# A four-layer graph network: graph 0's first attention row without the identity, graph 2's first layer placed earlier, and a new order of all steps

## The chip, the cores and the metric

The kernel runs on one core of a Trainium2 chip. Its engines are TensorE (PE, matrix products; weight loads are shown apart as PEld), VectorE (DVE), ScalarE (ACT), GpSimd (POOL) and SyncE (SP); the last two and ACT also start DMA transfers. Every engine takes its instructions in order, and an instruction that waits for a semaphore holds those behind it on the same engine. The metric is the time of one execution on the device, in microseconds; lower is better. The time before is the median of three runs.

## The reference

Sixteen independent graphs of 1024 nodes with 128 features pass through four layers. All four use the same 0/1 adjacency matrix of the graph, and each ends with a residual and a normalization:

```python
x = _layernorm(x + _L0_gnn_ref(x, adj, W, a))                     # one attention head, 128 wide
x = _layernorm(x + _L1_gnn_ref(x, adj, adj, W, a))                # 8 heads of 16, ELU at the end
x = _layernorm(x + _L2_gnn_ref(x, adj, rel_weights, self_w, ...)) # mean over neighbours, own norm
x = _layernorm(x + _L3_gnn_ref(x, adj, W))                        # 4 heads of 32, scores Wh.Wh
```

Layer 0 is the layer that the change touches most:

```python
H = X @ W;  s = H @ a_src;  t = H @ a_dst
e = leaky_relu(s[:, None] + t[None, :], 0.2)
attention = softmax(where(A > 0, e, -1e9));  out = relu(attention @ H)
```

The kernel writes the exponential of a leaky ReLU as a maximum of two products. With `most`, the largest t, each weight is proportional to max(R0[i], q[j]) times a factor of j alone, where R0[i] = exp(-0.8 max(s[i] + most, 0)) and q[j] = exp(0.8 (t[j] - most)). So a mask product needs a tile R0 that holds the row over i on all 128 partitions, a number q per partition, and the mask. Layer 1 does the same with eight heads.

## The kernel before, in words

The fast path is `tile_binary`; `tile_general` stands behind a branch that is taken only if the adjacency is not 0/1, and does not run here. A graph has eight masks (`m`, 128 source nodes by 1024 targets, 8-bit floats), which POOL loads and converts by DMA (L605).

`before0` loads the transposed features in two chunks (`xT`, L621), multiplies them with `w0c` (`products`, L393: W and, as extra columns, W a_src, W a_dst and -1/128), copies the result to `hd` on ACT (L629, L636), takes the largest t on DVE (L643) and over the partitions on POOL (L416), and forms `r` (L654, exponential at L660) and `q`. For graph 0 the tile R0 is made by 16 matmul records (L585) whose weights are columns of `r` and whose other operand is the identity matrix. For all other graphs the row goes through DRAM: a transpose with the identity (L498), a copy (L500), a store (L503) and a load to all partitions (L672). `layer0` then makes, for each half of the targets, eight mask products on DVE (L697, 128x512) and the sums on PE (L709), and divides, adds the residual and normalizes (`layernorm`, L438 to L486).

`before1` and `layer1` do the same for eight heads in two groups of four: 64 mask products of 128x1024 per graph (L849) and the sums (L857, four heads side by side in PE's columns). Graph 0's first four R tiles are again made by products with the identity (L585) and ACT copies (L810), the rest by DMA (L814). `last1` applies ELU, residual and norm. `layer2` sums over neighbours on PE with the mask as weights (L989) and has its own norm. `before3` prepares layer 3, and `layer3` computes scores on PE (L1139 for the missing edges, L1150), exponentials on ACT (L1221) and sums on PE (L1165; in the last graphs L1176 and L1187, with additions on DVE at L1243).

The order of the work is not that of the code. Every piece is a `step` with an engine, an estimated duration, a due time and the buffers that it reads and writes. `Plan.run` walks through time: per engine it takes, among the steps that can start within `WINDOW` of the first possible start, the one with the smallest due time, emits its instructions, and so fixes the engine's order. For PE a step of the same tiling mode as the last one (full, rows, 32 columns) counts as due `SAME` earlier. `lag` is the delay that the plan assumes until others see the result, for a DMA its landing. Pools hold a fixed number of places, and a step that needs a place waits until one is free. `plan.user("acc1", due, ...)` gives the turns on the one pair of accumulators that layers 0 and 1 share: graph 0's layer 0 (0), graph 1's (25), graph 0's layer 1 in two groups (99 and 154.5), graph 1's first group (228), graph 2's layer 0 (258), graph 1's second group (283.5), and so on, 129 apart.

The identity (`constants`, L512 to L535) is made in DRAM by three transfers that depend on each other, issued by ACT (L525): zeros, ones on the diagonal, and the load to `b_ident`. `far`, a scaled copy for layer 3, follows on DVE (L535). `weights` loads and prepares the weights.

Of the kernel before, what the change touches and what calls it, by code (L numbers as in the profile page):

```python
# [28 lines left out]
P = 128  # L29
HALF = 512  # L30
# [46 lines left out]
class Plan:  # L77
# [8 lines left out]
    SAME = 43.42  # L86
    WINDOW = {"DVE": 0.32, "ACT": 0.56, "POOL": 24.74, "SP": 1.21, "PE": 0.04}
    URGENT = 87.13
# [145 lines left out]
def tile_binary(  # L234
# [62 lines left out]
    LATER1 = 126.77  # L297
    LATER3 = -19.68
    LATERX = 258.97
# [43 lines left out]
    places("x1", 2, [P, NB, P])  # L343
    places("x2", 2, [P, NB, P])
    places("x3", 2, [P, NB, P])
# [40 lines left out]
    def products(xT, w, due, into, us, floor=0.0):  # L386
# [14 lines left out]
        step("PE", us, due - 42.13, emit, [xT, w], [out], holds=[into], floor=floor)  # L401
        return out, lambda: out.t.rearrange("p (k c) -> p k c", c=SLOT)[:, :, :cols]

    def turned(x_nat, chunk, due):

        pt, xT = Buf("wk", "pt"), Buf("xTc", "xTc")
        step(
            "PE", 0.44, due - 52.2, lambda: transposes(pt.t, [x_nat.t[:, chunk * HB + k, :] for k in range(HB)]),
            [(x_nat, chunk), xT, identity], [pt],
        )  # L410
        step("ACT", 0.47, due + 19.59, lambda: nc.scalar.copy(xT.t, pt.t[:, :HALF]), [pt], [xT])
        return xT

    def over_partitions(v, op, shape, due, op_us=None):
        got = little(f"all{shape[1]}", shape)
        step("POOL", 0.6 if op_us is None else op_us, due - 256.91, lambda: nc.gpsimd.partition_all_reduce(got.t, v.t, P, op), [v, heated], [got], lag=0.6)  # L416
        return got

    def sums(y, half, tot, due):

        ks = slice(half * HB, (half + 1) * HB)
        step(
            "DVE", 0.62, due - 13.18, lambda: nc.vector.tensor_reduce(tot.t[:, ks], y.t[:, ks, :], AX.X, ALU.add),  # L423
            [(y, half)], [(tot, half)],
        )

    def layernorm(y, tot, due, rest=None, half=None):
# [16 lines left out]
        step("DVE", 0.1, due - 236.47, minus_mean, [tot_of, rest] if rest else [tot_of], [off])  # L444
# [7 lines left out]
        for pair in pairs:  # L452
            step(
                "ACT", 1.05, due + pair - 6.55, lambda pair=pair: square(pair), [off, (y, pair // 2)], [(squared, pair), junk]
# [5 lines left out]
            "ACT", 0.17, due - 65.07,  # L460
# [4 lines left out]
            "ACT", 0.17, due - 217.77,  # L465
# [3 lines left out]
            "DVE", 0.1, due - 138.7,  # L469
# [12 lines left out]
        step("DVE", 0.35, due - 474.69, newton, [about, var, off], [rstd, shift])  # L482
# [7 lines left out]
        for pair in pairs:  # L490
            step("ACT", 0.77, due + pair - 6.15, lambda pair=pair: apply(pair), [shift, rstd], [(y, pair // 2)])

    def rows_everywhere(r, flat, count, due):
# [4 lines left out]
            "PE", 0.2, due + 269.89, lambda: nc.tensor.transpose(pt.t[: count * NB, :P], flat(r.t), ident), [r, rT, identity], [pt]  # L498
        )
        step("ACT", 0.2, due - 282.01, lambda: nc.scalar.copy(rT.t[: count * NB, :], pt.t[: count * NB, :P]), [pt], [rT])  # L500
        step(
            "SP", 0.5, due - 721.27,
# [7 lines left out]
    def load(due, into, out, in_, part=None):  # L510
        step("SP", 0.45, due - 48.89, lambda: nc.sync.dma_start(out=out(), in_=in_), [], [(into, part)], lag=3.0)

    def constants(due):
        none = Buf("z", "none")
        step("DVE", 0.2, due - 932.32, lambda: nc.vector.memset(none.t[:, :P], 0.0), [], [none])
        for n, (out_, in_) in enumerate(
# [7 lines left out]
                "ACT", 0.1, due - 1208.47,  # L524
                lambda out_=out_, in_=in_: nc.scalar.dma_start(out=out_(), in_=in_()),  # L525
                [none] if n == 0 else [square_of] if n == 2 else [], [square_of] if n < 2 else [identity], lag=2.5,
            )
            if n == 0:

                def table():  # L530
                    nc.scalar.preload_act_table_set("natural_log_exp_and_others")
                    nc.scalar.activation(warm, warm, AF.Exp)

                step("ACT", 1.5, due - 840, table, [], [heated])
        step("DVE", 0.2, due - 74.81, lambda: nc.vector.tensor_scalar(far, ident, -FAR, None, ALU.mult), [identity], [farther])  # L535
        step(
            "POOL", 0.5, due - 989.31, lambda: nc.gpsimd.partition_all_reduce(warm, warm, P, bass_isa.ReduceOp.add),
# [3 lines left out]
    def weights(due):  # L541
        t = Buf("z", "prep")
        load(due - 1904.86, w0c, lambda: w0c.t[:, :P], w0, 0)
        load(due - 1680.94, t, lambda: t.t[:, : 2 * P], a0.rearrange("k o -> (k o)").partition_broadcast(P), 0)
# [8 lines left out]
        step("DVE", 0.9, due - 280.19, joined0, [(t, 0)], [w0c, (t, 1)])  # L553
        due += 90
        u = Buf("z", "prep")
        load(due - 65.18, w1c, lambda: w1c.t[:, :P].rearrange("p (h o) -> p h o", h=H1), w1.rearrange("h f o -> f h o"), 0)
        load(due + 386.63, u, lambda: u.t[:, : 2 * P], a1.rearrange("h k o -> (h k o)").partition_broadcast(P), 0)
# [10 lines left out]
        step("DVE", 1.1, due - 112.88, joined1, [(u, 0)], [w1c, (u, 1)])  # L568
        due += 60
        load(due - 435.76, w2c, lambda: w2c.t[:, P:], w2[1], 0)  # L570
        load(due - 69.23, u, lambda: u.t[:, 4 * P : 5 * P], self_w, 2)
        load(due - 442.33, rows["self_b"], lambda: rows["self_b"].t, self_b.partition_broadcast(P))
        pt = Buf("wk", "pt")
        step("PE", 0.2, due + 255.16, lambda: transposes(pt.t, [u.t[:, 4 * P : 5 * P]]), [(u, 2), identity], [pt])
# [1374 lines left out]
```

## Time and profile before

| what | value |
|---|---|
| median of 3 runs | 2183.86 us (2183.72 to 2184.57) |
| the profiled execution, own time | 2186.08 us |
| its span in the profile | 2184.2 us |
| PE busy, DVE busy, ACT busy | 2046.5, 1945.6, 1761.7 us |
| mean granted PE clock | 0.978 |
| first mask product of layer 0 | 24.67 us after the span's start |
| first mask product of layer 1 | 67.75 us |
| layer 1's mask products (L849), 1024 of them | 1248.2 us of DVE, 1278 ns each as recorded |

A line of a timeline gives start, duration, engine, source line, operation, output and inputs with their shapes, how many instructions are merged, and in brackets how long the engine was idle before and what ended that idle time. A line by stretch gives the length, busy time and number of instructions for PE, PEld, DVE, ACT and POOL, then the granted PE clock as a share, the DMA engines' busy share and GB/s. A line of the list of waits gives who waited for whom, with the sum in us, how often, and the longest. Records of PE overlap, since matmuls are pipelined, so the start of the next group tells more than a group's duration.

### The profile page before, as it was taken

How to read it: one execution, taken by the hardware profiler on the slowest of the kernel's cores; microseconds unless marked ns; L12 is line 12 of the kernel's file. 1: busy time of each engine (PE TensorE's matmuls, PEld its weight loads, DVE VectorE, ACT ScalarE, POOL GpSimd, SP SyncE). 2: the span in 40 equal slices, each digit the busy share in tenths (PEclk: the TensorE clock that was granted, in tenths of full speed). 3: DMA queues.
4: the chain of work that ended last, by engine and by line, in shares of the span. 5: the costliest groups of instructions: out<-in, count | busy, mean ns of one | idle time of the engine just before them, and what ended most of it. 6: DMA issues, size and time to landing. Idle time of an engine off the chain costs nothing.

```text
span 2184.2 us, 55248 instructions
## 1 busy us (share of the span) xinstructions
PE 2046.5 (94%) x23344; PEld 982.0 (45%) x23344; DVE 1945.6 (89%) x2883; ACT 1761.7 (81%) x4360; POOL 109.8 (5%) x185
## 2 busy tenths in 40 slices
PE   6757999999999999999999999999999999999877
PEld 5414445453544545354454435345443635442422
DVE  5799999999999999999999999999999999999444
ACT  3414769889797979979797997979799797979987
POOL 1000000000000000000000000000000000000000
PEclk9888999999999999999999999999999999999989
DMA  7140220412323041232204122220413222020000
GB/s 114 49 98 20 65 60 15 101 38 86 43 79 57 18 100 34 86 43 93 44 18 101 33 91 38 93 43 18 101 33 91 38 91 38 2 78 11 11 2 22
DMA packets 81282, 119.97 MB, mean 55 GB/s; under 512 B 7560, under 2 KB 59136, under 8 KB 81024
## 3 DMA queue, kind: packets, MB, share of 16 engines
q1 hardware_dynamic: 62160, 99.43, 13.7%
q0 software_dynamic: 18432, 16.79, 9.5%
q8 instruction: 184, 3.01, 0.6%
q14 instruction: 74, 0.61, 0.1%
q10 hardware_dynamic: 432, 0.13, 0.0%
HBM read 157.61 MB, written 9.04 MB: 76 GB/s over the span
## 4 chain that ended last, share of the span: by engine, by line
PE 47%; DVE 29%; issue 15%; ACT 5%; DMA 2%; POOL 1%; POOLq 0%; SPq 0%; DVEq 0%; ACTq 0%
DVE z L849 18%; PE acc L709 10%; PE acc L1165 10%; PE acc L857 9%; PE wk L1150 6%; PE wk L384 3%; PE wk L393 3%; PE wk L1139 2%; POOL all L416 1%; PE wk L1062 1%; DMA R<-rows 1%; DVE tot L423 1%; PE acc L1176 1%; DVE rest L957 1%; DVE x L964 1%
## 5 line engine op out<-in xcount | busy, mean ns | idle before, releaser
L849 DVE SCALAR_TENSOR_TENSOR z<-R,q,m 128x1024 f32<-128x1024 f32 x1024 | 1248.2, 1278 | 23.0 <-PE acc L857 20.7
L857 PE MATMUL acc<-z,hh 128*32 128x512 f32 x4096 | 516.7, 613 | 59.4 <-DVE z L849 57.0
L1221 ACT ACTIVATE z<-wk,low 128x1024 f32<-128x1024 f32 x448 | 477.8, 1108 | 29.8 <-PE wk L1150 27.5
L1165 PE MATMUL acc<-z,hh 128*32 128x512 f32 x1792 | 454.3, 598 | 1.7 <-ACT z L1221 1.7
L1165 PE MATMUL acc<-z,ones 128*32 128x512 f32 x1792 | 454.3, 598 | 0.0
L448 ACT ACTIVATE junk<-x,off 128x128 f32<-128x128 f32 x640 | 257.1, 402 | 42.8 <-DVE off L442 26.7
L1150 PE MATMUL wk<-whT,turn 32*64 32x512 f32 x3952 | 287.0, 615 | 0.0
L857 PEld LDWEIGHTS acc<-z,hh 128*32 128x32 f32 x4096 | 117.5, 111 | 367.0 <-issue 226.8
L486 ACT ACTIVATE x<-x,shift,rstd 128x128 f32<-128x128 f32 x640 | 264.6, 487 | 6.8 <-DVE shift L480 6.6
L709 PE MATMUL acc<-hd,z 128*128 128x129 f32 x2048 | 252.3, 279 | 8.2 <-DVE z L697 4.3
L709 PEld LDWEIGHTS acc<-hd,z 128*128 128x128 f32 x2048 | 240.7, 194 | 38.4 <-DVE z L697 16.7
L1165 PEld LDWEIGHTS acc<-z,hh 128*32 128x32 f32 x1792 | 89.6, 109 | 213.2 <-issue 181.7
L697 DVE SCALAR_TENSOR_TENSOR z<-R,q,m 128x512 f32<-128x512 f32 x240 | 165.9, 744 | 22.0 <-DMA R<-rows 22.0
L989 PEld LDWEIGHTS <-m 128*128 128x128 fp8e5 x3072 | 178.4, 98 | 14.4 <-issue 14.4
L989 PE MATMUL wk<-y,m 128*128 128x128 bf16 (+1 forms) x2976 | 175.7, 220 | 0.9 <-DVE y L975 0.9
L1129 ACT ACTIVATE gap<-m,neg_one 128x512 bf16<-128x512 fp8e5 x240 | 171.4, 716 | 0.0
L1139 PEld LDWEIGHTS <-far 32*32 32x32 bf16 x4096 | 37.1, 87 | 217.0 <-issue 214.3
L448 ACT ACTIVATION_READ_ACCUMULATOR junk<-x,off 128x1 f32 x640 | 120.8, 189 | 0.0
L1165 PEld LDWEIGHTS acc<-z,ones 128*32 128x32 f32 x1792 | 89.5, 109 | 53.1 <-issue 53.1
L1139 PE MATMUL wk<-gap,far 32*32 32x512 bf16 x3784 | 106.7, 386 | 5.7 <-ACT R L1221 5.4
L605 POOL DMA_DIRECT2D m<-in_adj_dram x128 | 68.4, 539 | 723.6 <-ACT gap L1129 698.3
L660 ACT ACTIVATE r<-r 128x8 f32<-128x8 f32 x16 | 3.3, 208 | 119.7 <-DVE r L654 119.7
(158 smaller groups left out, 2120.7 us busy)
## 6 DMA issues: line engine op xcount, KB each, us to landing
R<-rows SPq DMA_DIRECT2D x139, 512.0 KB
m<-in_adj_dram POOLq DMA_DIRECT2D x128, 128.0 KB, 5.3
xT<-in_xT_dram SPq DMA_DIRECT2D x32, 256.0 KB
x<-in_x_dram SPq DMA_DIRECT2D x16, 512.0 KB
out_dram<-x SPq DMA_DIRECT2D x15, 512.0 KB
rows<-rT SPq DMA_DIRECT2D x16, 32.0 KB
out_dram<-x SPq DMA_DIRECT2D x2, 256.0 KB
z<-in_L_gnn_a_dram SPq DMA_DIRECT2D x2, 128.0 KB
```

The source lines that it names most:

```text
L448: nc.scalar.activation(junk.t, y.t[:, k, :], AF.Square, bias=off.t[:, k : k + 1], accum_out=squared.t[:, k : k + 1])
L486: nc.scalar.activation(y.t[:, k, :], y.t[:, k, :], AF.Identity, bias=shift.t[:, k : k + 1], scale=rstd.t[:, k : k + 1])
L697: nc.vector.scalar_tensor_tensor(z.t[:, (j % 2) * HALF : (j % 2 + 1) * HALF], in0=R0.t[:, cols], scalar=q.t[:, j : j + 1], in1=m[j].t[:, c ...
L709: nc.tensor.matmul(av[k // 2].t.rearrange("p (k c) -> p k c", k=2)[:, k % 2, : P + 1], lhsT=z.t[:, at : at + P], rhs=hd.t[:, j, : P + 1], ...
L849: nc.vector.scalar_tensor_tensor(z.t, in0=G["R"][h].t, scalar=q.t[:, j, h : h + 1], in1=m[j].t, op0=ALU.max, op1=ALU.mult)
L857: nc.tensor.matmul(av[half].t[32 * c : 32 * c + 32, :], lhsT=hh.t[:, j, at : at + 32], rhs=zs[c].t[:, half * HALF : (half + 1) * HALF], st ...
L989: nc.tensor.matmul(ps.t[:, k * SLOT : k * SLOT + part.stop - part.start], lhsT=m[j].t[:, rows_i], rhs=y2.t[:, j, part], start=j == 0 and n ...
L1129: nc.scalar.activation(gap.t, m[j].t if b == B - 1 else m[j].t[:, cols], AF.Square, bias=neg_one, accum_out=squares[:, at : at + 1], satur ...
L1139: nc.tensor.matmul(sc[h // 2].t[c * 32 : (c + 1) * 32, (h % 2) * HALF : (h % 2 + 1) * HALF], lhsT=far[rows_r, rows_r], rhs=gap.t[rows_r, c ...
L1150: nc.tensor.matmul(sc[h // 2].t[r * 64 : (r + 1) * 64, (h % 2) * HALF : (h % 2 + 1) * HALF], lhsT=turns[j // HB].t[rows_h, j % HB * P + r ...
L1165: nc.tensor.matmul(av[g].t[at : at + 32, :], lhsT=lhsT, rhs=z.t[:, h, :], start=j == 0, stop=j == NB - 1,)
L1221: lambda g=g, sc=sc, zs=zs: nc.scalar.activation(zs[g].t.rearrange("p h n -> p (h n)"), sc[g].t, AF.Exp, bias=low.t, scale=S3),
```

## The change

It does five things.

- Graph 0's R0 is computed straight from the features: a matmul whose weights are the column W a_src, repeated 128 times, against the transposed features gives s on all partitions in PSUM (`straight`); DVE adds the maximum, ACT takes the exponential. The tile lies in the pool `R`, no longer in PSUM, and the identity is not used for it.
- The identity's three transfers are issued by SP, behind the loads of the features, and the lags that the plan assumes for them are longer.
- Graph 2's layer 0 gets the turn after graph 1's on the accumulators (due 50), ahead of graph 0's layer 1. Its masks are loaded after the maximum of graph 1.
- The pools `x1`, `x2` and `x3` of two places each become one pool `x` of five.
- Graph 0's layer 1 starts a group of four heads only when all four R tiles of the group are written, and the R tiles of its second group are loaded in the order that a tile of the first group allows. Nearly every due time, `SAME`, `WINDOW`, `URGENT`, the `LATER` constants and the period of the due times change too.

```diff
-    SAME = 43.42
-    WINDOW = {"DVE": 0.32, "ACT": 0.56, "POOL": 24.74, "SP": 1.21, "PE": 0.04}
-    URGENT = 87.13
+    SAME = 95.7
+    WINDOW = {"DVE": 0.33, "SP": 0.35, "ACT": 0.47, "POOL": 29.09, "PE": 0.02}
+    URGENT = 85.48
...
-    LATER1 = 126.77
-    LATER3 = -19.68
-    LATERX = 258.97
+    LATER1 = -3.66
+    LATER3 = 290.53
+    LATERX = 593.46
...
-    places("x1", 2, [P, NB, P])
-    places("x2", 2, [P, NB, P])
-    places("x3", 2, [P, NB, P])
+    places("x", 5, [P, NB, P])
...
             step(
-                "ACT", 0.1, due - 1208.47,
-                lambda out_=out_, in_=in_: nc.scalar.dma_start(out=out_(), in_=in_()),
-                [none] if n == 0 else [square_of] if n == 2 else [], [square_of] if n < 2 else [identity], lag=2.5,
+                "SP", 0.4, -900 + 4 * n + 36.19,
+                lambda out_=out_, in_=in_: nc.sync.dma_start(out=out_(), in_=in_()),
+                [none] if n == 0 else [square_of] if n == 2 else [], [square_of] if n < 2 else [identity], lag=(3.0, 4.0, 4.0)[n],
             )
...
-                    after, [m], lag=(5.0 + j if j < 4 else 1.6 + 1.05 * j) if b == 0 else 8.0 + 1.05 * j if b == 1 else 5.6,
-                    floor=0.0 if b < 2 else 124 * b - 110 + 5 * j,
+                    after, [m], lag=(4.5 + 1.2 * j if j < 4 else 1.0 + 1.05 * j) if b == 0 else 8.7 + 1.05 * j if b < 3 else 5.6,
+                    floor=0.0 if b < 3 else 124 * b - 110 + 5 * j,
                 )
-        if b == 1:
-            masks(range(NB), due + 40, [G["after"]])
+        if b in (1, 2):
+            masks(range(NB), due + 40, [graphs[b - 1]["most"]])
...
+            if b == 0:
+                step(
+                    "PE", 0.9, -700 + chunk - 130.27,
+                    lambda xT=xT, chunk=chunk: nc.tensor.matmul(
+                        straight.t[:, chunk * HALF : (chunk + 1) * HALF],
+                        lhsT=w0c.t[:, P : P + 1].to_broadcast([P, P]),
+                        rhs=xT.t,
+                        start=True,
+                        stop=True,
+                    ),
+                    [xT, w0c], [(straight, chunk)],
+                )
...
-            R0 = G["R0"] = Buf("wk", "R0_0")
+            R0 = G["R0"] = Buf("R", "R0_0")
             for half in range(2):
+                cols = slice(half * HALF, (half + 1) * HALF)
                 step(
-                    "PE", 1.0, due - 320.62 + half - 13.03, row_by_products(lambda: r.t, R0, range(half * HB, half * HB + HB)), [r, identity], [(R0, half)]
+                    "DVE", 0.7, -900 + half - 574.39,
+                    lambda cols=cols: nc.vector.tensor_scalar(
+                        R0.t[:, cols], straight.t[:, cols], most.t, 0.0, ALU.add, ALU.max
+                    ),
+                    [(straight, half), most], [(R0, half)],
+                )
+                step(
+                    "ACT", 0.6, -900 + half + 2.31,
+                    lambda cols=cols: nc.scalar.activation(R0.t[:, cols], R0.t[:, cols], AF.Exp, scale=-(1.0 - SLOPE)),
+                    [], [(R0, half)],
                 )
...
-            plan.user("acc1", (25 if b == 1 else 129 * b) + half * 10, av, made)
+            plan.user("acc1", (25 if b == 1 else 50 if b == 2 else 129 * b) + half * 10, av, made)
...
-                [kept], [R], lag=2.0, floor=75.0 if b == 0 else 0.0,
+                [kept, *G["R"][h - G1 : h - G1 + 1]] if b == 0 else [kept], [R], lag=2.0,
...
-                            lambda j=j, c=c, z=z, f=weights: f(j, c, z), [G["R"][g * G1 + c], q, m[j]], [z],
+                            lambda j=j, c=c, z=z, f=weights: f(j, c, z), (G["R"][g * G1 : g * G1 + G1] if b == 0 else [G["R"][g * G1 + c]]) + [q, m[j]], [z],
...
-    PERIOD = 131.1
+    PERIOD = 136.19
...
-        at0 = 25 if b == 1 else at
+        at0 = 25 if b == 1 else 50 if b == 2 else at
```

## The prediction

> **What bounds the kernel now.** First the page: the busy sums, and the span in 40 slices of 54.6 us.
>
> ```profile
> PE 2046.5 (94%) x23344; PEld 982.0 (45%) x23344; DVE 1945.6 (89%) x2883; ACT 1761.7 (81%) x4360; POOL 109.8 (5%) x185
> ...
> PE   6757999999999999999999999999999999999877
> ...
> DVE  5799999999999999999999999999999999999444
> ...
> PEclk9888999999999999999999999999999999999989
> ```
>
> TensorE (PE) works 2046.5 of 2184.2 us. Its 137.7 us of idleness lie in the first four slices and the last three; the first stretch also has a lower granted clock. Next, busy time by stretch (columns: length, then busy us of PE, PEld, DVE, ACT, POOL, then PEclk, DMA share, GB/s). I cut at the first mask product of layer 0 (24.67), the end of graph 1's layer 0 (64.8), the end of graph 0's layer 1 (157), and graph 0's first scores of layer 3 (about 240).
>
> ```profile
> 0.00:24.67 24.67, 9.73 (x49) 8.84 (x49) 3.39 (x19) 6.62 (x23) 8.33 (x24) 0.86 0.86 142
> 24.67:64.80 40.13, 34.68 (x283) 33.70 (x284) 26.80 (x52) 18.54 (x72) 1.84 (x4) 0.96 0.44 68
> 64.80:157.00 92.20, 57.94 (x386) 21.72 (x388) 86.90 (x88) 24.03 (x70) 6.70 (x10) 0.83 0.36 86
> 157.00:240.00 83.00, 61.04 (x517) 40.20 (x513) 78.12 (x122) 47.38 (x149) 0.90 (x1) 0.86 0.06 18
> 240.00:1985.00 1745.00, 1721.26 (x20183) 822.69 (x20175) 1642.96 (x2432) 1495.09 (x3703) 88.76 (x144) 1.00 0.25 59
> 1985.00:2184.20 199.20, 161.89 (x1940) 54.89 (x1936) 107.45 (x174) 170.10 (x347) 3.24 (x3) 0.93 0.03 10
> ```
>
> PE idles 14.9, 5.5, 34.3 and 22.0 us in the first four (76.7 together), 23.7 in the long middle, 37.3 in the tail. From 64.8 to 240 VectorE (DVE) is the bound (165.0 of 175.2 us); in the middle PE is (98.6%). So a microsecond is won by giving PE work before 240, by closing the middle's small gaps, or in the tail.
>
> Third, the timeline of the front, DVE then ACT, and who waits in the first 25 us:
>
> ```profile
> 17.10 0.23 DVE L535 TENSOR_SCALAR far<-b_ident 128x128 bf16<-128x128 f32 x1 [9.93 <-DMA b_ident<-square]
> 18.10 0.15 DVE L643 TENSOR_REDUCE top<-hd 128x1 f32<-128x8 f32 x1
> 24.67 6.68 DVE L697 SCALAR_TENSOR_TENSOR z<-wk,q,m 128x512 f32<-128x512 f32 x10 [1.20 <-PE wk L585]
> 38.17 4.73 DVE L697 SCALAR_TENSOR_TENSOR z<-R,q,m 128x512 f32<-128x512 f32 x7 [0.47 <-DMA R<-rows]
> 12.95 0.33 ACTq L525 DMA_DIRECT2D b_ident<-square  x1
> 13.38 0.60 ACT L629 COPY hd<-wk 128x520 f32<-128x520 f32 x1
> 22.30 0.22 ACT L660 ACTIVATE r<-r 128x8 f32<-128x8 f32 x1
> ```
>
> ACT's copies stand behind its identity transfer, which waits for the one before; the maximum stands behind `far`, which waits for the identity; r's exponential stands behind graph 1's copies. Graph 1's own row arrives only at 38.17.
>
> **The change, part by part.** Durations are of this execution: span 2184.2, own time 2186.08, 2.2 above the median of 2183.86. I sum against 2186.08 and take 2.2 off at the end.
>
> *Front of graph 0.* Removed from the path: the identity, r's exponential, 16 products L585 (2.05 us), three DMA issues on ACT (0.33 to 0.35 each). Added: two matmuls of 512 columns (0.63 each by L1062) beside the copies, two DVE steps of 0.69 (L964, also from PSUM), two exponentials of 0.59 (L411's size). New path: products end 12.11 (8.71 + 3.40), last copies 0.8, so 13.0; maximum and all-reduce 0.63 (18.10 to 18.73), so 13.6; one DVE step and one exponential 1.3, some 0.4 of handover: first z at 15.3, not 24.67, that is 9.4 earlier. But masks 4 to 7 still wait for the maximum. Their four issues now took 3.9 to 8.2 us to land; issued 13.5 to 15.2, the last is there by 23.4, where z j=7 wants it at 15.3 + 7 x 0.68 = 20.1. That returns 3.3: I take 6 us (ends 0 and 9.4).
>
> *The identity behind it on SP.* SP issues it after four loads (2.6). The three transfers took 5.08, 6.42 and 4.43; with issues it lands near 18.9, not 17.1. SP waits between them, and graph 1's feature loads (13.33 now) stand behind: about +1 (0 to +3). The first users, graph 1's row transpose (24.77) and `far` (first scores, 240), cover it. If `far` or the weight preparation still stands before R0's steps on DVE, the 6 us are gone.
>
> Here a rule speaks against the change: the Trainium skill's "DMA: Bandwidth & Descriptors", Issuing engines are not separate DMA queues, says that a DMA started from another engine uses the same 16 engines, so only issue time is saved. By the rule, this edit is worth ACT's three issues, 1 us, and the sum below would be 5 us poorer at the first z. The rows show the larger price: ACT's first copy is at 13.32, right behind the issue that waited.
>
> *Graph 2's masks.* Eight issues move on POOL from 124.39 (4.25 us) to behind graph 1's (to 29.2). The all-reduce at 61.84 is the next that matters, so POOL covers them. The POOL-issued DMA takes 9.5% of 2184 us for 128 masks, 1.6 us each: 13 us more in a DMA system that is busy until about 41 us. Masks are then in by about 54, just before they are used; R0 of graph 1 competes with them and lands at 34 to 41 (38.17 now). So graph 1's layer 0 starts at 38 as now, and the 6 us are given back there.
>
> *Graph 2's layer 0.* It leaves 212 to 234 and comes before layer 1 of graph 0. A layer 0 takes about 18.5 us of wall (25.47 to 43.9), 16 x 0.68 + 1.9 = 12.8 us of DVE and 16.5 of PE. What covers it: now nothing of layer 1 can start until 67.75, because graph 0's chain (residual, norm, products, rows) takes 24 us from the end of its layer 0 at 43.9. With graph 1 at 38 to 56 and graph 2 at 56 to 74, DVE is done with graph 2's z by about 72, so layer 1 starts 4.5 us later (ends 0 and +9). The new rule that graph 0's layer 1 wants all four R rows costs up to 73.07 - 67.75 = 5.3 us, but those rows are then ready before 72; layer 2's products and others are not touched. Behind it, 157 to 240 loses 12.8 us of DVE in a stretch where DVE is 94% busy, but also PE's filler. If DVE sets the chain from layer 1's end to the first scores, the stretch shrinks by 12.8; if latency sets it, DVE makes ten more z of layer 1, whose PE work of 5 us is then done early. I take 8.5, between the two. Front in all: +4.5 - 8.5 = -4 (ends: +9 - 5 = +4; 0 - 13 = -13).
>
> *The new order in the middle.* Every due time, `SAME` and the windows differ. One period:
>
> ```profile
> 614.44:741.12 126.68, 125.07 (x1470) 60.40 (x1466) 118.86 (x177) 109.80 (x274) 6.66 (x11) 1.00 0.25 60
> 741.12:867.32 126.20, 124.81 (x1470) 60.38 (x1466) 119.13 (x177) 109.65 (x274) 6.66 (x11) 1.00 0.27 60
> 867.32:994.49 127.17, 125.07 (x1470) 60.40 (x1466) 118.85 (x177) 109.78 (x274) 6.66 (x11) 1.00 0.26 60
> ```
>
> PE idles 1.4 to 2.1 us per period. A group of L857 of 8 starts its successor after 0.97 us (629.76 to 630.73), one of 16 after 1.85 (636.75 to 638.60), so a separate run costs 0.09; there are 24 such runs between the 16 score runs. `SAME` at 95.7 for 43.42 favours merging; I take three or four merged runs, 0.3, and 0.1 of idleness: -0.4 us x 13.8 periods (1745 / 126.5) = -5.5. Ends: all idleness and eight merges, -2.1 x 13.8 = -29; and every period as the worst shown, 127.17 - 126.45, +0.7 x 13.8 = +10.
>
> *Tail and pool.* The order of the last 199 us changes too; no row says which way: 0, ends -10 and +10 (PE waits of 3 to 4 us, three of them, either way). Five shared residual tiles for six: a graph's three live about 170, 110 and 226 us of a 126.5 us period, 4.0 at a time on average: 0 (up to +4 if the fifth is late).
>
> Sum: 2186.08 - 4 - 5.5 = 2176.6; less 2.2, 2174.4. I say 2174.5.
>
> **Rivals.** *Front and middle both pay in full:* the 157 to 240 stretch shrinks by all 12.8 and the period by 0.8: -13 - 11 = -24, about 2160. For it: DVE's 94% there. Against: layer 3's preparation is a chain of small steps.
>
> *The front is given back, the order is neutral:* graph 1's row keeps the start at 38.17, the +4.5 cancels the stretch behind. About 2184. For it: that wait's releaser is a DMA. Against: 34.3 us of PE idleness that earlier work can use.
>
> *Slower:* the period grows, because in the new order layer 0's R row comes late in every period. Thirteen such waits of DVE sum to 21.5 us in the middle (`DVE z L697 <- DMA R<-rows: 21.5, 13, 2.4`), and in the periods where PE has no backlog it follows. At +0.3 a period the front's 4 us are eaten; at +0.7, with the front's bad end (+4), it is 2184 + 10 + 4 = 2198. Against it: DVE has 7.6 us of slack per period.
>
> **How the numbers follow.** A measurement of this kernel tells about 0.2% (4.4 us) from no change: faster is under 2179.5, slower over 2188.2. Forecast 0.42, its own range 2163 to 2182 (0.04 of it within 0.2%); both in full 0.18; given back 0.10; slower 0.30. So faster 0.38 + 0.18 = 0.56, same 0.14, slower 0.30. The range leaves out a third of the full case, below 2154, and a third of the slower case, above 2198.
>
> **What would show it.** Right: L697 first at 15 to 19; graph 1's at 36 to 40; six layer-0 halves before the first L849, which starts at 70 to 74; first scores by 240; PE idle before 240 at 70 to 74 us; period 126.1. Wrong: `far` or a mask before L697 with a DMA as releaser past 20; first scores after 248; a period off by over 0.5 us either way, which by 13.8 outweighs all of the front; or a tail other than 199 us by over 10.

## The result and the profile after

The changed kernel took 2195.64 us (median of 6 runs, 2193.01 to 2198.83), the kernel before 2183.76 us beside it on the same chip (6 runs). The ratio is 1.0059, with an interval of 1.0046 to 1.0071: 0.6% slower, where 0.4% faster was forecast. The profiled execution took 2194.87 us, its span is 2193.1 us. The medians differ by 11.9 us and the two profiled spans by 8.9, since the profiled execution of the kernel before was 2.3 us above its median and that of the changed one 0.8 below. Lines have moved: L697 is now L718, L709 L730, L849 L870, L857 L878, L393 L391, L535 L532, L525 L523, L672 L693.

Busy sums and slices of 54.8 us, from the page of the changed kernel:

```profile
PE 2049.4 (93%) x23332; PEld 982.7 (45%) x23332; DVE 1942.4 (89%) x2884; ACT 1749.1 (80%) x4361; POOL 117.6 (5%) x185
...
PE   4856799999999999999999999999999999999887
...
DVE  2799998999999999999999999999989999999544
...
PEclk7978899999999999999999999999999999999999
```

TensorE (PE) idles 143.7 us, 6.0 more than before, and is busy 2.9 us longer. In the first slice PE's digit fell from 6 to 4, that of VectorE (DVE) from 5 to 2 and the granted clock's from 9 to 7. By stretch, cut at the first mask product of layer 0, the first of layer 1, the end of graph 0's layer 1, the first scores, and ahead of the last 199.2 us:

```profile
0.00:20.66 20.66, 6.82 (x20) 4.67 (x20) 3.90 (x15) 4.29 (x11) 8.34 (x23) 0.89 0.88 124
20.66:98.47 77.81, 57.93 (x453) 56.45 (x454) 40.84 (x87) 40.08 (x148) 6.77 (x14) 0.83 0.52 102
98.47:190.00 91.53, 57.38 (x378) 21.72 (x377) 86.63 (x87) 20.70 (x64) 1.33 (x1) 0.81 0.13 47
190.00:270.50 80.50, 55.85 (x467) 27.32 (x467) 75.01 (x106) 41.02 (x119) 1.25 (x1) 0.81 0.12 40
270.50:1993.90 1723.40, 1706.50 (x20074) 816.81 (x20078) 1626.72 (x2414) 1471.69 (x3667) 97.93 (x144) 1.00 0.25 58
1993.90:2193.10 199.20, 164.93 (x1968) 55.77 (x1952) 109.28 (x178) 171.32 (x355) 1.98 (x3) 0.94 0.03 10
```

Layer 0 starts 4 us earlier than before (20.66 for 24.67), layer 1 starts 30.7 us later (98.47 for 67.75), the first scores come 29.7 us later (270.5 for 240.8). The stretch between the end of graph 0's layer 1 and the scores is 80.5 us long for 83.8: 3.3 shorter, not 8.5.

For a ledger of the whole I cut at the issue of graph 0's and graph 11's output, which both kernels have. First the kernel before, then the changed one:

```profile
0.00:401.30 401.30, 321.21 (x3060) 175.36 (x3064) 348.37 (x493) 225.51 (x621) 26.64 (x50) 0.92 0.30 66
401.30:1792.80 1391.50, 1374.69 (x16086) 664.33 (x16082) 1307.97 (x1948) 1206.94 (x3004) 73.23 (x121) 1.00 0.26 60
1792.80:2184.20 391.40, 350.63 (x4206) 142.34 (x4198) 289.29 (x444) 329.30 (x737) 9.89 (x14) 0.96 0.11 26
```

```profile
0.00:429.70 429.70, 331.14 (x3131) 177.11 (x3131) 353.83 (x499) 231.71 (x633) 26.97 (x51) 0.88 0.28 63
429.70:1810.90 1381.20, 1372.28 (x16098) 664.55 (x16095) 1304.73 (x1948) 1195.76 (x3004) 82.10 (x121) 1.00 0.26 60
1810.90:2193.10 382.20, 345.99 (x4126) 141.07 (x4126) 283.83 (x439) 321.63 (x726) 8.53 (x13) 0.97 0.10 25
```

Front +28.4, middle -10.3, tail -9.2: together +8.9, the whole difference of the spans. The counts say more. Ahead of graph 0's output the new order does 5.5 us more of DVE's work and 71 more PE instructions; the tail has 5.5 us and 80 fewer. So I read some 5 to 6 us of the front's loss and of the tail's gain as one piece of work counted on the other side. PE's idleness went from 80.1 to 98.6 us in the front, from 16.8 to 8.9 in the middle and from 40.8 to 36.2 in the tail. The rest of the front's loss, 9.9 us, is PE busy for longer: it has the 71 instructions more, and its granted clock there is 0.88 for 0.92.

Where the front goes wrong, in the timeline of the changed kernel:

```profile
10.90 0.17 DVE L654 TENSOR_REDUCE top<-hd 128x1 f32<-128x8 f32 x1 [4.64 <-ACT hd L640]
...
11.38 4.25 POOL L602 DMA_DIRECT2D m<-in_adj_dram  x8
...
11.26 2.82 SPq L706 DMA_DIRECT2D x<-in_x_dram  x1
14.18 1.73 SPq L620 DMA_DIRECT2D xT<-in_xT_dram  x1
16.00 0.51 SPq L523 DMA_DIRECT2D b_ident<-square  x1
...
17.50 0.49 DVE L560 TENSOR_TENSOR z<-z,w1c 128x128 f32<-128x128 f32 x2 [6.44 <-DMA w1c<-in_L_gnn_W_dram]
...
20.66 0.75 DVE L718 SCALAR_TENSOR_TENSOR z<-R,q,m 128x512 f32<-128x512 f32 x1 [0.76 <-ACT q L696]
34.31 0.23 DVE L532 TENSOR_SCALAR far<-b_ident 128x128 bf16<-128x128 f32 x1 [12.90 <-DMA b_ident<-square]
...
32.87 2.09 PE L391 MATMUL wk<-w0c,xT 128*128 128x131 f32 x8 [19.75 <-DMA xT<-in_xT_dram]
36.37 2.08 PE L391 MATMUL wk<-w0c,xT 128*128 128x131 f32 x8 [1.41 <-DMA xT<-in_xT_dram]
38.25 5.40 PE L730 MATMUL acc<-hd,z 128*128 128x129 f32 x40
...
55.11 4.07 DVE L718 SCALAR_TENSOR_TENSOR z<-R,q,m 128x512 f32<-128x512 f32 x6 [3.84 <-DMA R<-rows]
```

The maximum is 7.2 us earlier (10.90 for 18.10). It releases not only graph 0's masks 4 to 7 but, behind them on POOL, graph 1's eight, all at 11.4 to 23.3 us. In that time SP's queue holds graph 0's rows of x (512 KB, issued at 11.26), the first half of graph 1's features (256 KB, 14.18) and the identity (64 KB, 16.00). Before, the features were issued at 13.33 and the rows behind them, at 14.38; the new order has the rows in front. The features are in use 18.7 us after their issue (they took 4.4 before), the identity 18.3 (at most 4.2 before: issued at 12.95, `far` at 17.10). PE, in order, stands 19.75 us at the features with graph 0's sums behind them; DVE stands 12.90 us at `far` with 15 of graph 0's 16 mask products behind it. Graph 1's row lands at 55.11, not 38.17.

### The profile page after: what moved, and what is told of

The parts are those of the page before. It is cut to its first block, busy times and chain, and to the rows that moved or that the text cites. A ratio compares the mean times of both kernels' runs of the same rounds, so it can differ in the third digit from the quotient of the medians.

```text
span 2193.1 us, 55270 instructions
## 1 busy us (share of the span) xinstructions
PE 2049.4 (93%) x23332; PEld 982.7 (45%) x23332; DVE 1942.4 (89%) x2884; ACT 1749.1 (80%) x4361; POOL 117.6 (5%) x185
## 4 chain that ended last, share of the span: by engine, by line
PE 64%; DVE 20%; ACT 11%; DMA 3%; issue 1%; SPq 0%; POOL 0%; DVEq 0%; ACTq 0%; POOLq 0%
PE acc L878 15%; DVE z L870 13%; PE acc L1186 11%; PE acc L730 9%; PE wk L1171 8%; PE wk L1010 7%; PE wk L391 5%; PE wk L382 4%; ACT x L484 3%; PE wk L1160 3%; ACT z L1242 2%; ACT junk L446 1%; DVE tot L421 1%; PE wk L1083 1%; ACT R L1242 1%
## 5 line engine op out<-in xcount | busy, mean ns | idle before, releaser
L870 DVE SCALAR_TENSOR_TENSOR z<-R,q,m 128x1024 f32<-128x1024 f32 x1024 | 1244.3, 1277 | 21.7 <-PE acc L878 20.0
L878 PE MATMUL acc<-z,hh 128*32 128x512 f32 x4096 | 516.7, 618 | 59.3 <-DVE z L870 57.2
L1186 PE MATMUL acc<-z,hh 128*32 128x512 f32 x1792 | 435.3, 596 | 1.7 <-ACT z L1242 1.7
L1186 PE MATMUL acc<-z,ones 128*32 128x512 f32 x1792 | 435.3, 596 | 0.0
L878 PEld LDWEIGHTS acc<-z,hh 128*32 128x32 f32 x4096 | 112.5, 111 | 366.4 <-issue 214.3
L730 PE MATMUL acc<-hd,z 128*128 128x129 f32 x2048 | 252.6, 279 | 7.1 <-ACT x L751 6.7
L730 PEld LDWEIGHTS acc<-hd,z 128*128 128x128 f32 x2048 | 241.6, 194 | 37.4 <-ACT x L751 19.8
L718 DVE SCALAR_TENSOR_TENSOR z<-R,q,m 128x512 f32<-128x512 f32 x256 | 176.7, 743 | 5.7 <-DMA R<-rows 5.0
L1186 PEld LDWEIGHTS acc<-z,ones 128*32 128x32 f32 x1792 | 95.2, 109 | 67.4 <-issue 67.4
```

Source lines behind the costliest of these rows:

```text
L718: nc.vector.scalar_tensor_tensor(z.t[:, (j % 2) * HALF : (j % 2 + 1) * HALF], in0=R0.t[:, cols], scalar=q.t[:, j : j + 1], in1=m[j].t[:, c ...
L730: nc.tensor.matmul(av[k // 2].t.rearrange("p (k c) -> p k c", k=2)[:, k % 2, : P + 1], lhsT=z.t[:, at : at + P], rhs=hd.t[:, j, : P + 1], ...
L870: nc.vector.scalar_tensor_tensor(z.t, in0=G["R"][h].t, scalar=q.t[:, j, h : h + 1], in1=m[j].t, op0=ALU.max, op1=ALU.mult)
L878: nc.tensor.matmul(av[half].t[32 * c : 32 * c + 32, :], lhsT=hh.t[:, j, at : at + 32], rhs=zs[c].t[:, half * HALF : (half + 1) * HALF], st ...
L1186: nc.tensor.matmul(av[g].t[at : at + 32, :], lhsT=lhsT, rhs=z.t[:, h, :], start=j == 0, stop=j == NB - 1,)
```

## The experiments

All runs but the sixth to the eighth freeze an order: the plan is made, its steps are collected, named groups of them are moved, and only then are the instructions emitted. With no group moved the order is that of the changed kernel; the fifth, ninth and eleventh run start from a new plan. A name such as z1_0_1_0_2 gives graph, group, mask and head.

```diff
-            s.emit()
+            order.append(s)
...
+        for names, after in self.moves:
+            moved = [s for s in order if s.tag in names]
+            order = [s for s in order if s.tag not in names]
+            at = max(n for n, s in enumerate(order) if s.tag in after) + 1
+            order[at:at] = moved
+        for s in order:
+            s.emit()
```

Event times of one profiled execution of each kernel (us): graph 1's features in use, first mask product of layer 0 of graph 1, first of layer 1, first scores, graph 0's output, then middle and tail as cut above, and the ratio of the medians to the kernel before with its interval:

| run | features | layer 0 of graph 1 | layer 1 | scores | output 0 | middle | tail | ratio |
|---|---|---|---|---|---|---|---|---|
| before | 17.9 | 38.2 | 67.8 | 240.8 | 401.3 | 1391.5 | 391.4 | 1 |
| after | 32.9 | 55.1 | 98.5 | 270.5 | 429.7 | 1381.2 | 382.2 | 1.0059 (1.0046 to 1.0071) |
| 1 far later | 34.2 | 56.1 | 99.1 | 270.7 | 429.9 | 1381.3 | 382.2 | 1.0048 (1.0033 to 1.0062) |
| 2 masks later | 24.4 | 45.8 | 87.8 | 261.6 | 420.8 | 1380.1 | 381.5 | 1.0007 (0.9995 to 1.0020) |
| 3 rows of x later | 20.0 | 45.5 | 87.4 | 261.1 | 420.4 | 1380.0 | 382.1 | 1.0015 (1.0003 to 1.0027) |
| 4 all | 20.4 | 43.2 | 85.3 | 259.3 | 418.6 | 1380.3 | 384.9 | 0.9997 (0.9984 to 1.0011) |
| 5 also graph 2 back | 20.7 | 42.4 | 72.9 | 264.0 | 418.7 | 1381.0 | 382.1 | 0.9997 (0.9985 to 1.0008) |
| 9 four groups moved | 20.7 | 40.7 | 68.8 | 259.0 | 413.7 | 1380.1 | 383.3 | 0.9995 (0.9984 to 1.0005) |
| 11 two more | 22.3 | 43.5 | 72.5 | 258.4 | 413.1 | 1380.6 | 382.9 | 0.9979 (0.9968 to 0.9989) |

**First run: `far` behind graph 2's layer 0.**

```diff
+    plan.moves = [(("far",), ("z0_2",))]
```

> The changed kernel with every engine's order kept, except that the one DVE step that makes far from the identity stands behind graph 2's layer-0 mask products instead of behind the very first mask product. In the changed kernel DVE waited 12.9 us at it. Theory A (the early masks hold up everything that SP loads: graph 1's features, landed at 32.9, and the identity, at 34.3): graph 0's masks products now run from 20.7 on, but PE's next work is graph 1's products, which stand ahead of graph 0's sums and wait for those features, so the first layer-1 mask product moves from 98.5 by 3 us at most and the time is 2190 to 2196. Theory B (it is the place of far in DVE's order that costs): the 12.9 us come back, first layer-1 product near 86, time 2180 to 2184.

2195.13 us, as theory A said; graph 0's output at 429.9. The 12.90 us that DVE stood at `far` cost nothing: without it DVE has masks and row, but PE still stands at graph 1's features.

**Second run: graph 1's eight masks behind graph 1's maximum on POOL.**

```diff
+    plan.moves = [(("masks1",), ("most1",))]
```

> The changed kernel with every engine's order kept, except that on POOL graph 1's eight mask loads are issued behind graph 1's all-reduce instead of ahead of it, so they wait for graph 1's features to have arrived. Theory A (the masks' transfers starve SP's loads): features of graph 1 land near 20 instead of 32.9, the identity near 22 instead of 34.3, graph 0's sums start near 25 instead of 38.3, the first layer-1 mask product near 84 instead of 98.5, and the time is 2178 to 2184. Theory C (SP's own queue is what is slow, since graph 0's 512 KB of residual rows stand ahead of them): features and identity land 4 us earlier at most, time 2189 to 2195.

2186.95 us, 8.7 less; the features are in use at 24.4, 8.5 us earlier, and output 0 is 8.9 earlier. Both theories missed: A expected features near 20 and 2178 to 2184 us, C at most 4 us.

**Third run: graph 0's rows of x behind graph 1's features and the identity on SP.**

```diff
+    plan.moves = [(("x0",), ("xT1_1", "identity2"))]
```

> The changed kernel with every engine's order kept, except that on SP the load of graph 0's residual rows (512 KB, issued at 11.3) stands behind graph 1's features and the identity. Theory C (SP's own order): features land near 19, identity near 20, first layer-1 mask product near 84, time 2178 to 2184. Theory A (the masks take the DMA engines): SP's queue moved some 45 KB per us beside the masks, so 512 KB less ahead bring features and identity about 8 to 11 us earlier, time 2184 to 2190, and moving the masks (the run beside this) brings more.

2186.43 us, 9.2 less; features at 20.0, near what theory C said, with a time in theory A's range; that moving the masks brings more was wrong. Either move alone takes back most of the 11.9 us, so the delay needs both: the large transfer in front in SP's queue, and the masks that keep the DMA engines busy (a share of 0.99 from 11.3 to 36.4 us in the changed kernel).

**Fourth run: both, with `far` late and the preparation of w1 behind graph 0's mask products.**

```diff
+    plan.moves = [(("masks1",), ("most1",)), (("x0",), ("xT1_1", "identity2")),
+                  (("far",), ("z0_2",)), (("joined1",), ("z0_0",))]
```

> Both moves together, masks of graph 1 behind its all-reduce and the residual rows behind features and identity, and on DVE far behind graph 2's layer-0 products and the preparation of layer 1's weights behind graph 0's. If the front's loss of 28 us by graph 0's output (429.7 against 401.3 in the kernel before) is nothing but late loads, first mask product near 15, graph 0's sums from about 22, first layer-1 product near 78 and time 2170 to 2177, below the kernel before. If placing graph 2's layer 0 first costs by itself (theory D), the first layer-1 product stays over 88 and the time over 2183.

2183.41 us, 12.2 less than the changed kernel, and level with the kernel before. The first mask product is at 15.1:

```profile
12.81 1.41 DVE L677 TENSOR_SCALAR R<-wk,all 128x512 f32<-128x512 f32 x2 [1.76 <-PE wk L629]
15.11 2.74 DVE L718 SCALAR_TENSOR_TENSOR z<-R,q,m 128x512 f32<-128x512 f32 x4 [0.75 <-ACT q L696]
...
20.36 2.08 PE L391 MATMUL wk<-w0c,xT 128*128 128x131 f32 x8 [7.67 <-DMA xT<-in_xT_dram]
22.90 2.09 PE L391 MATMUL wk<-w0c,xT 128*128 128x131 f32 x8 [0.45 <-DMA xT<-in_xT_dram]
24.78 4.90 PE L730 MATMUL acc<-hd,z 128*128 128x129 f32 x40
```

Little comes of it: in PE's order graph 1's products stand ahead of graph 0's sums (L730), which start at 24.8, where they started at 25.5 before the change. Layer 1 still starts 17.5 us late and output 0 comes 17.3 us late. The time is over theory D's 2183, layer 1's 85.3 between the 78 and the 88 of the two theories; that would make the placement of graph 2 the price. The next run speaks against that.

**Fifth run: graph 2's layer 0 back at its old turn, its masks loaded late (the lines for its masks are not shown), planned anew, with the moves of the fourth run (without `far`).**

```diff
-            plan.user("acc1", (25 if b == 1 else 50 if b == 2 else 129 * b) + half * 10, av, made)
+            plan.user("acc1", (25 if b == 1 else 129 * b) + half * 10, av, made)
...
-        at0 = 25 if b == 1 else 50 if b == 2 else at
+        at0 = 25 if b == 1 else at
```

> The changed kernel with graph 2's layer 0 back at its old turn on the accumulators (258) and its masks loaded late, the order planned anew, and with graph 1's masks, graph 0's rows of x and the preparation of w1 moved back as in the fourth run. Theory D (the placement delays layer 1 by its own length and nothing pays it back in front of the first scores): first mask product of layer 1 at 68 to 73, first scores at 240 to 247, graph 0's output at 400 to 408. Its rival (the front is late for another reason, such as the straight row or the late identity): layer 1 still past 80, output past 415. For the middle, theory O (the new order of all steps makes the periods shorter, whatever graph 2 does): 1380 to 1383 between the outputs of graphs 0 and 11, tail 382 to 386, end at 2162 to 2177 with D. Theory G (the middle is shorter only because graph 2's layer 0 is already done): 1389 to 1393 and 390, end at 2180 to 2190.

Layer 1 starts at 72.9, as expected, but the output of graph 0 does not move (418.7), nor the time (2183.27). Theory D falls for these two orders: layer 1 starts 12.4 us later with graph 2 in front, the scores come 4.7 earlier and the output at the same time. Since the order was planned anew, the two runs differ in more than the placement; what it is worth by itself is not shown. Theory G falls: the middle is 1381.0 without the placement. Its gain belongs to what the fifth run keeps, the new due times and constants and with them the pool of five (theory O). The stages of the fifth run:

```profile
0.00:418.70 418.70, 334.87 (x3126) 180.51 (x3126) 353.86 (x499) 231.83 (x633) 26.49 (x51) 0.89 0.29 65
418.70:1799.70 1381.00, 1372.62 (x16103) 664.48 (x16087) 1304.72 (x1948) 1195.81 (x3005) 82.13 (x121) 1.00 0.25 60
```

DVE idles 64.8 us ahead of the output (fourth run 64.7, before 52.9): 12 of the 17.4 us. The other 5.5 are DVE's work that the tail no longer has. TensorE idles only 3.7 us more than before ahead of that output and is busy 13.7 longer, at a granted clock of 0.89 for 0.92; no run shows how much of the 17.4 us is due to that.

**Sixth run: the kernel before with the placement alone**, its masks behind graph 1's maximum, and the pool of five that it needs.

```diff
-    places("x1", 2, [P, NB, P])
-    places("x2", 2, [P, NB, P])
-    places("x3", 2, [P, NB, P])
+    places("x", 5, [P, NB, P])
...
-        if b == 1:
-            masks(range(NB), due + 40, [G["after"]])
+        if b in (1, 2):
+            masks(range(NB), due + 40, [graphs[b - 1]["most"]])
...
-        at0 = 25 if b == 1 else at
+        at0 = 25 if b == 1 else 50 if b == 2 else at
```

> The kernel before with the placement alone: graph 2's layer 0 at turn 50, its masks loaded behind graph 1's maximum, and the one pool of five residual tiles that this needs; everything else, the identity row and all due times, as before. Theory D: layer 1 starts at 83 to 92 (67.8 now), first scores 256 to 265, graph 0's output at 416 to 426. Rival (the 157 to 240 stretch shrinks by about 8.5, as predicted): scores at 236 to 248, output at 397 to 409. For the middle, theory O: still 1389 to 1393, so an end of 2196 to 2210 with D; theory G: 1379 to 1384, tail 380 to 386, an end of 2176 to 2192 with D.

2317.69 us, ratio 1.0601 (1.0582 to 1.0621); the middle is 1513.1. Both theories on the middle are off by 120 us: with these due times the plan finds another, bad order. Only the early part can be read: with its row there at 36.9, graph 1's layer 0 is followed by graph 2's, and layer 1 starts at 70.3, 2.5 us later than before. The scores (257.6) and output 0 (414.1) are as late as theory D has them, or nearly, but DVE idles 92.5 us ahead of that output (52.9 before), so the bad order may be what delays them.

**Seventh and eighth run: `SAME` alone**, 43.42 in the changed kernel and 95.7 in the kernel before.

```diff
-    SAME = 95.7
+    SAME = 43.42
```

> The changed kernel with one number put back: SAME is 43.42 for 95.7, so that PE prefers to stay in one tiling mode less strongly; the order is planned anew. Theory S (the middle's gain is fewer changes of mode, by SAME): the middle goes back from 1381 to 1386 to 1392 us, with one separate group of column runs more per period. Rival (gain from the other due times or from the placement): the middle stays at 1378 to 1384. The front is not its question: output of graph 0 at 420 to 435 by both.

> The kernel before with one number changed: SAME is 95.7 for 43.42, planned anew. Theory S: the middle falls from 1391 to 1381 to 1388, end 2174 to 2182. Rival: the middle stays within 1389 to 1394 or grows, because the other due times were made for 43.42.

2320.58 and 2369.56 us, ratios 1.0628 (1.0610 to 1.0645) and 1.0847 (1.0829 to 1.0865), middles of 1550.4 and 1503.6. Neither theory said this. It settles nothing on why the middle is shorter; in both kernels this value of `SAME` was of use only with the rest of its set.

**Ninth run: the fifth, with four groups of steps moved**, at DVE's longest waits between 25 and 130 us.

```diff
+    plan.moves += [(("far",), ("z0_1",)), (("row1",), ("rexp1",)),
+                   (("z1_0_0_0_1", "z1_0_0_0_2", "z1_0_0_0_3", "z1_0_0_1_0", "z1_0_0_1_1"), ("z1_0_0_0_0",)),
+                   (("rd1_0_0", "x2_0_0"), ("z1_0_1_0_2",))]
```

> The order of the fifth run, frozen, with four groups of steps moved: the scaled copy far behind graph 1's layer 0; the transpose, copy and store of graph 1's row directly behind the exponential; five mask products of graph 0's layer 1 ahead of graph 1's norm (which VectorE waited 5.7 us for); graph 0's first division behind three mask products of the second group (2.7 us waited). Theory W (what remains of the front's loss is VectorE standing at steps that the plan put too early, and VectorE sets the pace from layer 1 to the first scores): those waits go, first scores at 252 to 258 instead of 264.0, graph 0's output at 406 to 413 instead of 418.7, middle and tail as they were (1381 and 382), end at 2169 to 2177 and faster than both kernels. Rival (another chain sets the first scores, or the lower granted clock of TensorE in that stretch): output at 416 to 420, end at 2179 to 2184.

Output 0 at 413.7, 5.0 earlier, between the two theories; the median is 2182.60. The profiled execution, 2178.89 us, was the fastest of its twelve. The fifth run's timeline first, then the ninth's:

```profile
72.87 1.28 DVE L870 SCALAR_TENSOR_TENSOR z<-R,q,m 128x1024 f32<-128x1024 f32 x1 [0.20 <-ACT R L831]
79.89 0.17 DVE L468 TENSOR_SCALAR var<-squared 128x8 f32<-128x8 f32 x1 [5.74 <-ACT junk L446]
...
90.30 0.26 DVE L804 TENSOR_REDUCE top<-e 128x8 f32<-128x64 f32 x1 [0.69 <-ACT e L791]
```

```profile
78.52 0.16 DVE L468 TENSOR_SCALAR var<-squared 128x8 f32<-128x8 f32 x1
...
88.72 0.26 DVE L804 TENSOR_REDUCE top<-e 128x8 f32<-128x64 f32 x1 [6.97 <-ACT e L791]
```

The wait of 5.74 us is gone, and 6.97 us appear at the next step of the same chain of graph 1: squares, norm, transposes, products, maximum. The mask products that were taken forward ran out in front of it.

**Tenth run: the third transfer of the identity issued by ACT**, in the changed kernel.

```diff
-                lambda out_=out_, in_=in_: nc.sync.dma_start(out=out_(), in_=in_()),
+                lambda out_=out_, in_=in_, n=n: (nc.scalar if n == 2 else nc.sync).dma_start(out=out_(), in_=in_()),
```

> The changed kernel, its order frozen, with the third transfer of the identity issued by ACT instead of SP, nothing else. Theory Q (the transfer was slow because it stood in SP's queue behind 512 KB of x and 256 KB of features): it lands 4 to 7 us after its issue, far starts before 24 us instead of 34.3. Theory E (the sixteen engines are shared and the masks hold them, whichever queue the transfer is in): it lands 12 us or more after its issue, far starts past 28 us. The second half of graph 1's features, still in SP's queue, lands at about 33 by both.

```profile
14.62 0.34 ACTq L523 DMA_DIRECT2D b_ident<-square  x1
...
21.57 0.23 DVE L532 TENSOR_SCALAR far<-b_ident 128x128 bf16<-128x128 f32 x1
```

`far` starts at 21.57 without a wait: the transfer took at most 7.0 us, where it took 18.3 in SP's queue under the same masks. Theory Q is right, E wrong. The first half of graph 1's features, which stood ahead of the identity in SP's queue, is in use at 33.2, as late as ever. The only execution took 2193.63 us, with output 0 at 428.7: as in the first run, it had cost little that the identity was late.

**Eleventh run: the ninth, with graph 0's first sums of layer 1 ahead of graph 1's products on PE, and four more mask products ahead of graph 1's maximum on DVE.**

```diff
+    plan.moves += [(("z1_0_0_2_0", "z1_0_0_2_1", "z1_0_0_2_2", "z1_0_0_2_3"), ("z1_0_0_1_3",)),
+                   (("s1_0_0_0",), ("z1_0_0_1_1",))]
```

> The ninth run, frozen, with two more groups moved: the sums of graph 0's first mask product of layer 1 ahead of graph 1's transposes and products on TensorE, and four more mask products of layer 1 ahead of graph 1's maximum on VectorE, which waited 7.0 us for it. Theory W (VectorE's waits between 68 and 100 us are what is left): the wait at the maximum falls under 3 us, the sixteenth mask product of layer 1 at 93 to 96 instead of 99.3, first scores at 253 to 256, graph 0's output at 407 to 411, profiled end at 2170 to 2174, median 2 to 6 us below the kernel before. Rival (graph 1's chain, now later by the moved sums, sets the second layer 1 and the first scores): output at 412 to 416, median within 2 us of the kernel before.

```profile
82.97 7.26 DVE L870 SCALAR_TENSOR_TENSOR z<-R,q,m 128x1024 f32<-128x1024 f32 x6
92.08 0.26 DVE L804 TENSOR_REDUCE top<-e 128x8 f32<-128x64 f32 x1 [1.85 <-ACT e L791]
```

The wait at the maximum is 1.85 us. From the first to the seventeenth mask product of layer 1 it takes 25.7 us instead of 30.5 (22.3 before the change). Since the features came 1.6 us later in this profile (22.3), layer 1 started 3.7 later and the output only 0.6 earlier, at 413.1, short of the 407 to 411 of theory W. The median is 2178.48 us against 2182.62: ratio 0.9979 (0.9968 to 0.9989), 0.2% less and the one version that is faster than both kernels. The profiled spans of the ninth and eleventh run differ by 0.5 us only (2177.1 and 2176.6), so the profiles don't show where the 4 us between their medians come from.

## Why the prediction was wrong

**The identity behind it on SP, and graph 1's masks: the step that failed.** I priced SP's waits between the transfers (graph 1's features "about +1 (0 to +3)"), and the earlier masks only for what they do to graph 0 (3.3 us). I didn't ask what else the earlier maximum triggers, nor what the new order puts in front of the features in SP's queue. The maximum puts twelve mask loads on the DMA engines at the time of SP's transfers, and graph 0's rows of x now stand ahead of these. Before, features and identity had landed by 17.9, ahead of the first of those masks at 18.57. Measured: features +15.0 us instead of +1, identity at 34.3 instead of 18.9. Moving the masks, or the rows of x, takes back 8.7 or 9.2 us; both, with `far` and w1 late, 12.2. I also misread a row: the 4.43 us that I took for the identity's third transfer are the load of graph 1's features. The identity took at most 4.2 us, which changes little.

**Graph 1's layer 0 "starts at 38 as now".** It starts at 55.1; with the loads mended at 43.2, 5 us late.

**Front of graph 0.** I summed 15.3 without obstacles, and the fourth run has 15.1, partly by luck. The products start at 6.3 us, not 8.71, and the all-reduce is done at 11.5, not 13.6. But the two matmuls that make s, 0.63 us each in my sum, are four records over 2.75 us there; DVE waits 1.76 us for them, and `q` then comes behind the row. Two errors of some 2 us cancel. And PE's order makes nothing of the early product, as the fourth run shows. In the changed kernel the weight preparation stood before R0's steps (6.44 us at w1c), which I had named as the case where the gain is gone, and `far` stood behind the first product (12.90 us).

**Graph 2's layer 0.** I took +4.5 for layer 1 and -8.5 for the stretch behind, net -4. Fourth against fifth run: +12.4 at layer 1's start, -4.7 at the scores, -0.1 at output 0. Net 0, as in the rival "the front is given back", though its mechanism was another; the two orders differ in more than the placement. In the sixth run, on the old due times, layer 1 starts only 2.5 us later. So what the placement costs depends on the order around it, and its price by itself stays open.

**What I left out: a new order has its own stalls in the front.** Even with the loads mended DVE idles 12 us more ahead of graph 0's output, at steps that the plan put where they must wait: for graph 1's row (5.0 us in the fourth run, 0.5 before), for the division of graph 0's first group (5.6 over all such, 1.7 before), for graph 1's norm (5.74 in the fifth). The ninth and eleventh run moved steps away from these waits, and 5.6 us came back at output 0. The 11.8 us that are left there are not explained: in the eleventh run DVE still idles 59.2 us ahead of output 0 for 52.9, and has 5.5 us more work.

**The middle: right in sign, and more than twice the size.** -10.3 us over eleven periods, 0.94 a period where I took 0.4. I expected 0.3 of that from merged runs of PE and 0.1 from less idleness. It is the reverse: PE busy -2.4, idle -7.9 over the eleven periods, that is 0.2 and 0.7 us a period. PE's waits in the middle, before and after:

```profile
PE acc L857 <- DVE z L849: 6.0, 11, 0.6
PE wk L393 <- ACT xTc L411: 5.0, 11, 0.5
PE wk L498 <- DVE degrees L1006: 4.2, 11, 0.4
PE acc L709 <- DVE z L697: 1.5, 4, 0.7
```

```profile
PE wk L391 <- ACT xTc L409: 5.3, 6, 0.9
PE wk L391 <- ACT z L1242: 2.2, 11, 0.3
PE acc L730 <- ACT x L751: 1.3, 2, 0.7
```

The waits for layer 1's mask products and for `degrees` are gone. The lines sum to 16.7 and 8.8 us, all of PE's idleness there. Why this order has them covered is read from the traces only; no run isolated it.

**The tail** of the ledger gained 9.2 us, but 5.5 us of DVE's work are merely done earlier. It is also some 190 us longer than the 199 us that I gave 0, so the two can't be set side by side; from the issue of the fourteenth output to the end it is 138.6 us before and 136.4 after.

**The rival that ended slower** had the right sign and the wrong place. The row of layer 0 did not come late in every period: DVE's wait for it in the middle fell from 18.0 us in 11 waits to 1.1 in 2. And the 18.0 us had cost PE little: its wait behind those products, L709, was 1.5 us. The pool, costed at 0, was not tried by itself.

## What to carry to other kernels

When an edit makes one result earlier, list everything that waits for that result, in every queue, and look at what is in flight at the new time: here one maximum released twelve loads into transfers that used to be finished. A wait of an engine that isn't the bound (12.90 us of DVE at `far`) may cost nothing, and the order made by this tuned set of constants could not be taken apart one constant at a time (one `SAME` put back or forward cost 125 and 185 us); freezing the order and moving steps gave experiments that could be read.

## What the runs showed of the hardware

- With the masks running (POOL's queue), a 64 KB load in SP's queue took 18.3 us, and at most 7.0 us from ACT's queue, in one execution each. In the prediction I weighed the rule of the Trainium skill's "DMA: Bandwidth & Descriptors", Issuing engines are not separate DMA queues, by which another engine saves issue time alone. This transfer contradicts it: standing in SP's queue, behind 512 KB of x and 256 KB of features, cost it 11 us. That queues also slow each other shows in the second run: with graph 1's masks out of POOL's queue at that time, the features in SP's were in use at 24.4 us instead of 32.9.
- The first 25 us vary from execution to execution: in kernels whose instructions agree up to there, graph 1's features were in use at 20.7 and at 22.3 us (ninth and eleventh run), its layer 0 started at 40.7 and 43.5, and layer 1 at 68.8 and 72.5.
